# A hybrid of conv attention, causal attention and a recurrence: the first steps in a stated order, the provisional factor from 31 tiles, and W x of the last tile's first 384 queries in the final chain

## The chip, the cores and the metric

One NeuronCore of a Trainium2 chip runs the whole program. The metric is the device time of one execution in microseconds; the profile adds the span from the first to the last instruction of one execution.

## The reference, cut to what matters

The input `x` is (4, 128, 64, 64), float32: four images of 128 channels and 4096 positions.

```python
x = x + conv_attn(gn(x))          # q, k: 64 channels, v: 128; softmax(q k) over all 4096 positions, no mask
t = tokens(x)                     # (4, 4096, 128)
t = t + attn(ln(t))               # one head of 128, causal, scale 1/sqrt(128)
Wx = ln(t) @ W.T                  # then per channel over all 4 x 4096 tokens:
Wx = (Wx - mean) * rsqrt(var + 1e-5) * gamma + beta
y[l] = sigmoid(Wx[l] + y[l-1] @ V.T)    # scan over the 4096 tokens; V orthogonal
out = t + y
```

Mean and variance of `Wx` need every token of every image, so the scan can't get its final factor and offset before the last tile of the last image has passed both attentions.

## The kernel before, in words

`fast_kernel` does the work; it leaves a flag, and `general_kernel`, a plain version, runs afterwards only if the flag says that the result may not be trusted (`ok`, `good`, `wrong` at its end, L1281 to L1297).

**Tiles.** Tokens lie on the free axis in tiles of 512 queries (`QT`), eight per image (`NQ`). Scores are made for pairs of 128 keys: one unit is (image, layer, tile, pair). `score` (L1038 on) issues the two score products `ps` on TensorE (PE) and the exponential `s` on ScalarE (ACT); `product` issues the product with the values, `av`, and on VectorE (DVE) the running sum `total`. In the causal layer the diagonal blocks are cut by a select on GpSimd (POOL), L1073. `s` has three buffers.

**Start.** `gn_stats` gives the group norm's mean and factor of image 0. `keys0` then makes per tile: the normalised `xg` (DVE, L681), an addition of the value bias to X on POOL (L683), the joint projection `pk` of queries and keys (PE, L686), the keys `k` (ACT, L689) and the queries `QR` (DVE for image 0, L696), the split of the keys in a high and a low part (`kh` L699, `K` L700 and L703), and the values `pv` (PE, L707) with their copy (ACT, L708). `query0` splits the queries in the same way (`qh` L717, `q` L720 and L721). `xg` has two buffers, the small PSUM pool (`misc`) two.

**Between tiles.** Generators of the side work stand in lists, and `step` advances them, one step per unit. A scheduler then orders the instructions of each engine. The last part, `last_part`, stands under `tc.manual_schedule`, where the engines keep the program's order.

**End.** The last tile of image 3 is done in two parts, 384 queries (`LAST`) and 128. `ffn` makes, for each tile, the deviation of every token (`deviations`, `rstd`), spreads it along the free axis (`spread`: seven small copies and a transpose on DVE), multiplies it onto `W x` (`pw`, PE L824; product L825) into `WX`, and gathers statistics. From all tiles but the last 128 queries a provisional ("guess") gain and offset are made (`scale(9, "guess")`); with these the states ahead of each chunk of the recurrence take their first step (`first_step`, ACT L594). `last_part` finishes the last 128 queries, their statistics (`scale(15, "all")`) give the final gain and offset, and the chains of the recurrence start (`seed`, `advance`, L1187, L1202, L1203). Each chunk is warmed up from ten tokens ahead (`WARM`), and `BEHIND` chunks of the last image take their first step with the final factor.

`idle` issues matmuls whose result nobody reads.

Of the kernel before, what the change touches and what calls it, by code (L numbers as in the profile page):

```python
# [25 lines left out]
F32 = mybir.dt.float32  # L26
AF = mybir.ActivationFunctionType
ALU = mybir.AluOpType
# [446 lines left out]
def fast_kernel(  # L475
# [103 lines left out]
        nc.gpsimd.tensor_tensor(dst, dst, mhalf[:, :n], ALU.pow)  # L579

    first = []
    BEHIND = P // CHUNK[-1] - 1

    def shifted(gain, less, base, name):
        bias = const.tile([P, 1], F32, name=f"bias_{name}")
# [10 lines left out]
    with ExitStack() as actx:  # L596
# [75 lines left out]
        def keys0(b, c):  # L672

            if c == 0:
                K0[b] = kv.tile([P, N], F32R, tag="K0", name=f"K0_{b}")
                QR[b] = qr_tile(f"QR_{b}")
                V0[b] = WX[B - 1].rearrange("p l s t -> p (l s t)").rearrange("p (n c) -> p n c", c=C)
            xn = tmp.tile([P, QT], F32, tag="x", name=f"xg_{b}_{c}", bufs=2)
            gmv, grs = gn[b]
            xt = X[b][:, ts(c, QT)]  # L680
            nc.vector.tensor_scalar(xn, xt, gmv[:, 0:1], grs, ALU.subtract, ALU.mult)  # L681

            nc.gpsimd.tensor_scalar(xt, xt, B0v, None, ALU.add)  # L683
            yield
            pk = misc(f"pk_{b}_{c}")
            nc.tensor.matmul(pk, lhsT=W0qk.rearrange("p h o -> p (h o)"), rhs=xn, start=True, stop=True)  # L686
            k = tmp.tile([P, QT], F32, tag="k", name=f"k_{b}_{c}")
            low, up = slice(0, CQ), slice(CQ, P)
            nc.scalar.activation(k[up, :], pk[up, :], AF.Identity, bias=B0qk[up, :])  # L689
            half, col = divmod(c, NQ // 2)  # L690
            rows = QR[b][ds(half * CQ, CQ), ts(col, QT)]
            if b:

                nc.scalar.activation(rows, pk[low, :], AF.Identity, bias=B0qk[low, :])
            else:
                nc.vector.tensor_scalar(rows, pk[low, :], B0qk[low, :], None, ALU.add)  # L696
            yield
            high = tmp.tile([P, QT], F32, tag="h", name=f"kh_{b}_{c}", bufs=2)
            nc.vector.tensor_scalar(high[up, :].bitcast(I32), k[up, :].bitcast(I32), HIGH, None, ALU.bitwise_and)  # L699
            nc.vector.tensor_tensor(K0[b][up, ts(c, QT)], k[up, :], high[up, :], ALU.subtract)  # L700
            if b:
                yield
            nc.scalar.copy(K0[b][low, ts(c, QT)], high[up, :])  # L703
            yield
            pv = misc(f"pv_{b}_{c}")
            for j in range(4):
                nc.tensor.matmul(pv[:, ts(j, P)], lhsT=xn[:, ts(j, P)], rhs=W0v, start=True, stop=True)  # L707
            nc.scalar.copy(V0[b][:, 4 * c : 4 * c + 4, :], pv.rearrange("p (j c) -> p j c", j=4))  # L708
            yield

        def query0(b, c):

            half, col = divmod(c, NQ // 2)
            rows = ds(half * CQ, CQ)
            src = QR[b][rows, ts(col, QT)]
            high = tmp.tile([P, QT], F32, tag="h", name=f"qh_{b}_{c}", bufs=2)
            nc.vector.tensor_scalar(high[rows, :].bitcast(I32), src.bitcast(I32), HIGH, None, ALU.bitwise_and)  # L717
            q = qp.tile([P, 2, QT], F32R, tag="q", name=f"q0_{b}_{c}")
            for h in range(2):
                nc.scalar.copy(q[ds(h * CQ, CQ), h, :], high[rows, :])  # L720
                nc.vector.tensor_tensor(q[ds((1 - h) * CQ, CQ), h, :], src, high[rows, :], ALU.subtract)  # L721
            Q[b, 0, c] = q
            yield

# [75 lines left out]
        def ffn(b, c, off, w):  # L800
            name = f"f_{b}_{c}_{off}"
            cols = ds(c * QT + off, w)
            src = X2[b][:, cols]
            if b < len(kept):
                nc.sync.dma_start(out=kept[b][:, cols], in_=src)
            yield
            if (b, c) == (B - 1, NQ - 1):
                pt = misc(f"pt_{name}")
                for j in range(w // P):
                    nc.tensor.transpose(pt[:, ts(j, P)], src[:, ts(j, P)], ident)  # L810
                tok = pt.rearrange("p (j c) -> p j c", c=C)
            else:
                tok = yield from turn(src, None, name, ("f", b, c, off))
            _, rstd = deviations(tok, w // P, 1e-5, name)
            yield
            pw = misc(f"pw_{name}")[:, :w]

            part = WX[b][:, :, ds((c * QT + off) // CHUNK[b], w // CHUNK[b]), :].rearrange("p l s t -> p s l t")

            def chunks(row):  # L820
                return row.rearrange("p (s l t) -> p s l t", l=CHUNK[b] // 2, t=2)

            rb = spread(rstd, name)
            nc.tensor.matmul(pw, lhsT=FWc, rhs=src, start=True, stop=True)  # L824
            nc.vector.tensor_tensor(part, chunks(pw), chunks(rb), ALU.mult)  # L825
            if w == QT:
                nc.vector.bn_stats(stats_f[:, b * NQ + c, :], WX[b][:, :, ts(c, QT // CHUNK[b]), :])
                yield
                return
            nc.vector.bn_stats(groups[:, 3:9], WX[b][:, :, ds(c * QT // CHUNK[b], LAST // CHUNK[b]), :])  # L830
            yield
            whole(("most",))
            gain, less = scale(9, "guess")
            scales["guess"] = gain, shifted(gain, less, Fb0, "guess")
            yield

        scales = {}

        def scale(n, name):

            mv = small.tile([P, 2], F32, name=f"mv_{name}")
            nc.vector.bn_aggr(mv, groups[:, :n])
            gain = const.tile([P, 1], F32, name=f"gain_{name}")
            rsqrt(gain, mv[:, 1:2], 1e-5, 1)
            less = const.tile([P, 1], F32, name=f"less_{name}")
            nc.vector.tensor_scalar(less, mv[:, 0:1], -1.0, None, ALU.mult)
            nc.vector.tensor_tensor(gain, gain, Fgamma, ALU.mult)
            return gain, less

        def most_stats():  # L850

            for k in range(NQ - 1):
                whole(("f", B - 1, k, 0))
            mv = small.tile([P, 2], F32, name="mv_most")
            nc.vector.bn_aggr(mv, stats_f.rearrange("p c s -> p (c s)"))
            nc.vector.tensor_copy(groups[:, 1:2], mv[:, 0:1])
            nc.vector.tensor_scalar(groups[:, 2:3], mv[:, 1:2], float(B * N - QT), None, ALU.mult)
            yield

        def last_tokens():  # L860
# [3 lines left out]
            scales["tok"] = tok = small.tile([P, C], F32, name="tok_last")  # L864
            nc.scalar.copy(tok, pt[:, :P])
            yield

        def last_part(av, pz, s):

# [9 lines left out]
                first_step(b, 0, NC[b] - 1, scales["guess"])  # L879
            rz = small.tile([P, 1], F32, name="rz")  # L880
            nc.vector.reciprocal(rz, pz[:, 0:1])
            ptok = wide[0][:, 0, :w]
            nc.tensor.matmul(ptok, lhsT=avs, rhs=W1v, start=True, stop=True)
            prz = wide[1][:, 0, :w]
            nc.tensor.matmul(prz, lhsT=rz.to_broadcast([P, P]), rhs=ident, start=True, stop=True)
            po = misc("po_last")[:, :w]
            nc.tensor.matmul(po, lhsT=W1v, rhs=avs, start=True, stop=True)
            idle(misc("idle_last"), 3)
            tok = scales["tok"]
            nc.vector.scalar_tensor_tensor(tok, ptok, rz, tok, ALU.mult, ALU.add)  # L890
            rzs = tmp.tile([P, QT], F32, tag="b", name="rzs")[:, :w]
            nc.scalar.copy(rzs, prz)
            for b in range(2, B):
                first_step(b, 0, NC[b] - 1 - (BEHIND if b == B - 1 else 0), scales["guess"])
            stats = small.tile([P, 6], F32, name="lst_last")
# [5 lines left out]
            nc.vector.scalar_tensor_tensor(rzs, rzs, GUARD, po, ALU.mult, ALU.mult)  # L901
            x2 = X2[B - 1][:, cols]
            nc.vector.scalar_tensor_tensor(x2, rzs, 1.0 / GUARD, xt, ALU.mult, ALU.add)
            pw = misc("pw_last")[:, :w]
            nc.tensor.matmul(pw, lhsT=FWc, rhs=x2, start=True, stop=True)
            prow = wide[0][:, 1, :w]
# [1 line left out]
            idle(misc("idle_last2"), 2)  # L908
            raw = tmp.tile([P, QT], F32, tag="a", name="raw_last")[:, :w]
            nc.scalar.copy(raw, pw)  # L910
            part = WX[B - 1][:, :, ds((N - P) // CHUNK[-1], P // CHUNK[-1]), :]
            nc.vector.tensor_tensor(
                part.rearrange("p l s t -> p s l t"),
                *[t.rearrange("p (s l t) -> p s l t", l=CHUNK[-1] // 2, t=2) for t in (raw, prow)], ALU.mult,
            )
            nc.vector.bn_stats(groups[:, 9:15], part)
            scales["all"] = scale(15, "all")

        def finish(b, layer, c, off, w, av, total):

# [117 lines left out]
        def score(i):  # L1038
            b, layer, c, off, w, u, n = units[i]
            if u == 0:  # L1040
                if off == 0:
                    begin_tile(b, layer, c)
                else:
                    put(("most",), most_stats())
                    put(("tok",), last_tokens())
                st[b, layer, c, off] = {}
            if (b, layer, c) == (0, 0, 0) and u % 2 == 0:
                whole(("k0", 0, u // 2))
            q = Q[b, layer, c]
# [89 lines left out]
            pass  # L1139
        for k in range(NQ):  # L1140
            put(("k0", 0, k), keys0(0, k))
        whole(("k0", 0, 0))
        put(("q0", 0, 0), query0(0, 0))
        for i in range(len(units) + 1):
            if i < len(units):
                score(i)
# [200 lines left out]
```

## Time and profile before

| | |
|---|---|
| Three runs | 2507.52, 2508.29, 2508.2 us; median 2508.2 |
| The profiled execution | 2507.61 us |
| Its span, first to last instruction | 2505.9 us |
| Around the span | 1.7 us |
| Mean granted TensorE clock | 0.997 |
| Busy: PE, DVE, ACT, POOL | 99%, 71%, 45%, 8% |
| Instructions | 22483 |

The profile comes from one execution. A row of the timeline gives start, length, engine, line, operation, what is written from what, shapes, and in brackets the idle time of the engine before the row with what ended it. "PEld" are weight loads. A float32 matmul is two rows of the trace, one of `K` and `q` in layer 0 (a rounded type) is one. The chain is followed back from the last instruction, each step to what released it. In the stretches, the number in brackets is the count of instructions and the columns after POOL are the granted clock, the DMA engines' share and GB/s.

### The profile page before, as it was taken

To read this page: it belongs to the slowest core of one execution; us is meant where nothing else is said; L and a number is where in the kernel's file an instruction comes from. 1 tells how busy PE (TensorE), PEld (TensorE's weight loads), DVE (VectorE), ACT (ScalarE), POOL (GpSimd) and SP (SyncE) were. 2 spreads that over 40 slices of the span, in tenths; PEclk is the share of its full clock that TensorE was granted. 3 is DMA by queue.
4 is the path that set the end of the run, shared out by engine and by line. 5 is a ranking of instruction groups with operands and counts; after the bars stand their busy time and mean duration, and the time that the engine had idled before them with its cause. 6 is when DMAs were issued, how large, how long until landed. Compare 5 with 4: busy or idle time off the path is not lost.

```text
span 2505.9 us, 22483 instructions
## 1 busy us (share of the span) xinstructions
PE 2469.1 (99%) x7341; PEld 1339.8 (53%) x7341; DVE 1779.4 (71%) x3580; ACT 1138.7 (45%) x1421; POOL 206.9 (8%) x281
## 2 busy tenths in 40 slices
PE   7999999999999999999999999999999999999997
PEld 4555554444555555444555555544455555544465
DVE  6776669655987667856687676876578676786667
ACT  4444444444444444445444444444444444443456
POOL 2010001210000100110000010121010000010000
PEclk9999999999999999999999999999999999999999
DMA  2000001100100000110010000101010000010023
GB/s 75 9 17 9 17 9 38 26 21 13 49 15 9 17 9 18 38 26 13 24 45 13 13 9 18 34 26 26 13 47 17 9 16 10 13 30 17 9 74 138
DMA packets 154079, 64.41 MB, mean 26 GB/s; under 512 B 136160, under 2 KB 136928, under 8 KB 152160
## 3 DMA queue, kind: packets, MB, share of 16 engines
q1 hardware_dynamic: 151344, 59.27, 8.8%
q10 hardware_dynamic: 2608, 3.61, 0.4%
q8 instruction: 60, 0.98, 0.2%
q14 instruction: 67, 0.55, 0.1%
HBM read 31.66 MB, written 31.20 MB: 25 GB/s over the span
## 4 chain that ended last, share of the span: by engine, by line
PE 91%; DVE 5%; ACT 2%; issue 1%; POOL 0%; DMA 0%; SPq 0%; DVEq 0%; POOLq 0%; ACTq 0%
PE av L1108 51%; PE ps L1064 19%; PE ps L1057 16%; PE pv L707 1%; PE pw_f L824 1%; PE po L956 1%; DVE total L1105 1%; PE pk L686 1%; PE pq L794 1%; ACT WX L1203 1%; ACT states L1203 0%; PE pz L1202 0%; ACT WXp L1203 0%; DVE o L941 0%; DVE rb L771 0%
## 5 line engine op out<-in xcount | busy, mean ns | idle before, releaser
L1105 DVE TENSOR_TENSOR total<-total,s 128x1024 f32<-128x1024 f32 (+5 forms) x809 | 882.6, 1094 | 538.3 <-ACT s L1066 290.2
L1108 PE MATMUL av<-s,WXp 128*128 128x512 f32 x2048 | 962.0, 592 | 0.0
L1066 ACT ACTIVATE s<-ps,shift 128x1024 f32<-128x1024 f32 x512 | 570.2, 1115 | 762.2 <-PE ps L1064 743.7
L1064 PE MATMUL ps<-q,K 128*128 128x512 f32 x2048 | 757.9, 492 | 1.4 <-DVE K L700 1.2
L1070 ACT ACTIVATE s<-ps,zero,R 128x512 f32<-128x512 f32 (+3 forms) x607 | 405.8, 719 | 513.4 <-PE ps L1057 507.8
L1108 PEld LDWEIGHTS av<-s,WXp 128*128 128x128 f32 x2048 | 384.3, 188 | 304.0 <-issue 262.8
L1064 PEld LDWEIGHTS ps<-q,K 128*128 128x128 f32 x2048 | 386.2, 189 | 289.9 <-issue 231.1
L1108 PE MATMUL av<-s,V 128*128 128x512 f32 (+3 forms) x1214 | 504.4, 538 | 0.3 <-POOL s L1073 0.3
L1057 PE MATMUL ps<-q,X 128*128 128x512 f32 (+3 forms) x1214 | 503.5, 537 | 0.0
L1057 PEld LDWEIGHTS ps<-q,X 128*128 128x128 f32 x1214 | 224.9, 190 | 236.3 <-issue 219.5
L1108 PEld LDWEIGHTS av<-s,V 128*128 128x128 f32 x1214 | 223.6, 190 | 229.9 <-issue 205.4
L579 POOL TENSOR_TENSOR rstd<-rstd,mhalf 128x4 f32<-128x4 f32 x32 | 32.4, 1012 | 1024.4 <-DVE rstd L578 1024.4
L1073 POOL TENSOR_SCALAR_AFFINE_SELECT s<-s 128x128 f32<-128x128 f32 x128 | 48.7, 385 | 540.9 <-ACT s L1070 540.0
L579 POOL TENSOR_TENSOR rstd_f<-rstd_f,mhalf 128x4 f32<-128x4 f32 (+1 forms) x32 | 47.3, 1480 | 382.8 <-DVE rstd_f L578 362.3
L683 POOL TENSOR_SCALAR X<-X,B0v 128x512 f32<-128x512 f32 x32 | 64.6, 2021 | 141.5 <-DVE xg L681 140.0
L786 DVE TENSOR_SCALAR V<-V,lmv,rstd 128x128 f32<-128x128 f32 x128 | 38.7, 345 | 37.0 <-POOL rstd L579 36.9
L721 DVE TENSOR_TENSOR q<-QR,qh 64x512 fp32r<-64x512 f32 x64 | 44.1, 688 | 6.8 <-PE ps L1064 5.6
L924 DVE TENSOR_TENSOR t<-total 128x512 f32<-128x512 f32 x64 | 44.0, 688 | 4.2 <-PE pfw L638 2.5
L926 DVE STREAM_TRANSPOSE tt<-t 128x512 f32<-128x512 f32 x64 | 45.2, 707 | 1.7
L939 DVE STREAM_TRANSPOSE rb<-z 128x512 f32<-128x512 f32 x64 | 44.8, 700 | 0.9
L941 DVE SCALAR_TENSOR_TENSOR o<-rb,av 128x512 f32<-128x512 f32 x64 | 43.6, 681 | 2.3
L932 DVE COPY side<-part 32x16 f32<-32x16 f32 (+1 forms) x256 | 41.3, 161 | 3.9
(187 smaller groups left out, 1233.6 us busy)
## 6 DMA issues: line engine op xcount, KB each, us to landing
turn<-t SPq DMA_DIRECT2D x32, 256.0 KB, 2.0
V<-turn SPq DMA_DIRECT2D x128, 64.0 KB, 2.6
turn_f<-t_f SPq DMA_DIRECT2D x31, 256.0 KB, 2.0
t_f<-turn_f SPq DMA_DIRECT2D x124, 64.0 KB, 2.6
X<-in_x SPq DMA_DIRECT2D x28, 256.0 KB, 4.7
kept<-X SPq DMA_DIRECT2D x24, 256.0 KB, 2.0
Y<-kept SPq DMA_DIRECT2D x6, 1024.0 KB, 7.7
out<-Y SPq DMA_DIRECT2D x5, 1024.0 KB, 6.0
```

Of the source, the lines that this page charges most:

```text
L579: nc.gpsimd.tensor_tensor(dst, dst, mhalf[:, :n], ALU.pow)
L683: nc.gpsimd.tensor_scalar(xt, xt, B0v, None, ALU.add)
L721: nc.vector.tensor_tensor(q[ds((1 - h) * CQ, CQ), h, :], src, high[rows, :], ALU.subtract)
L926: nc.vector.transpose(tt, t)
L939: nc.vector.transpose(rb, z[:, :k].unsqueeze(2).to_broadcast([P, k, 32]))
L1057: nc.tensor.matmul(ps[:, h, first[h] : w], lhsT=lhsT, rhs=q[:, off + first[h] : off + w], start=True, stop=True,)
L1064: nc.tensor.matmul(ps[:, h, :], lhsT=lhsT, rhs=q[:, k, :], start=k == 0, stop=k == 1)
L1066: nc.scalar.activation(s, ps, AF.Exp, bias=shift)
L1070: nc.scalar.activation(part, ps[:, h, first[h] : w], AF.Exp, scale=scale, bias=zero)
L1073: nc.gpsimd.affine_select(out=edge, in_=edge, pattern=[[1, P]], base=0, channel_multiplier=-1, compare_op=ALU.is_ge, fill=0.0,)
L1105: nc.vector.tensor_tensor(t, t, s[:, h, f:w], ALU.add)
L1108: nc.tensor.matmul(av[:, first[h] : w], lhsT=V[:, 2 * u + h, :], rhs=s[:, h, first[h] : w], start=u == 0 and h == 0, stop=2 * u + h == n - 1,)
```

## The change

Three parts.

1. The first steps of `keys0` and `query0` of image 0 are issued in a stated order under `tc.manual_schedule` for DVE, ACT and PE: `xg_0`, `xg_1`, then `pk_0` with its reads, the first half of the queries' split, the keys' split, the second half, `pv_0` with its copy, `xg_2`, and `pk_1` with its reads. For the very first tile the queries are read out of `pk` ahead of the keys.
2. The provisional gain and offset come from the 31 full tiles (`most_stats`) and no longer from the first 384 queries of the last tile as well. `most_stats` starts at unit 11 of these 384 queries instead of at the beginning of the last 128. `BEHIND` goes from 3 to 15, the chunks of the whole last tile.
3. For the 384 queries, `ffn` ends with `rstd` and the product `pw`, left in a PSUM bank of the `av` pool. The row of deviations is made in `last_part` by three matmuls of the broadcast `rstd` with the identity (`row`), copied by ACT (`rows`), and multiplied onto `pw` with the statistics behind it (`write_last`), ahead of the same two operations for the last 128. One idle matmul ahead of the last `av` takes the place of three behind `po`.

```diff
-    BEHIND = P // CHUNK[-1] - 1
+    BEHIND = QT // CHUNK[-1] - 1
...
+            for read in (queries, keys) if (b, c) == (0, 0) else (keys, queries):
+                read()
...
             for h in range(2):
                 nc.scalar.copy(q[ds(h * CQ, CQ), h, :], high[rows, :])
                 nc.vector.tensor_tensor(q[ds((1 - h) * CQ, CQ), h, :], src, high[rows, :], ALU.subtract)
+                if (b, c, h) == (0, 0, 0):
+                    yield
...
             _, rstd = deviations(tok, w // P, 1e-5, name)
             yield
+            if w < QT:
+                pw = ps_av.tile([P, QT], F32, tag="av", name=f"pw_{name}")[:, :w]
+                nc.tensor.matmul(pw, lhsT=FWc, rhs=src, start=True, stop=True)
+                scales["early"] = pw, rstd
+                yield
+                return
...
-            nc.vector.bn_stats(groups[:, 3:9], WX[b][:, :, ds(c * QT // CHUNK[b], LAST // CHUNK[b]), :])
-            yield
-            whole(("most",))
-            gain, less = scale(9, "guess")
-            scales["guess"] = gain, shifted(gain, less, Fb0, "guess")
...
             mv = small.tile([P, 2], F32, name="mv_most")
-            nc.vector.bn_aggr(mv, stats_f.rearrange("p c s -> p (c s)"))
+            gain, less = scale(mv, stats_f.rearrange("p c s -> p (c s)"), "guess")
+            yield
+            scales["guess"] = gain, shifted(gain, less, Fb0, "guess")
...
+        def write_last(off, w, row, pw):
+            part = WX[B - 1][:, :, ds((N - QT + off) // CHUNK[-1], w // CHUNK[-1]), :]
+            nc.vector.tensor_tensor(
+                part.rearrange("p l s t -> p s l t"),
+                *[t.rearrange("p (s l t) -> p s l t", l=CHUNK[-1] // 2, t=2) for t in (row, pw)], ALU.mult,
+            )
+            k = 9 if off else 3
+            nc.vector.bn_stats(groups[:, k : k + 6], part)
...
             nc.vector.reciprocal(rz, pz[:, 0:1])
+            idle(misc("idle_last0"), 1)
...
-            idle(misc("idle_last"), 3)
...
             nc.scalar.copy(rzs, prz)
+            pw_early, rstd_early = scales["early"]
+            row = wide[1][:, 1, :LAST]
+            for j in range(LAST // P):
+                nc.tensor.matmul(
+                    row[:, ts(j, P)], lhsT=rstd_early[:, j : j + 1].to_broadcast([P, P]), rhs=ident, start=True, stop=True
+                )
...
+            rows = tmp.tile([P, QT], F32, tag="r", name="rows_early")[:, :LAST]
+            nc.scalar.copy(rows, row)
+            write_last(0, LAST, rows, pw_early)
             pw = misc("pw_last")[:, :w]
...
-            nc.vector.bn_stats(groups[:, 9:15], part)
-            scales["all"] = scale(15, "all")
+            write_last(LAST, w, raw, prow)
+            scales["all"] = scale(mv, groups, "all")
...
-                    put(("most",), most_stats())
                     put(("tok",), last_tokens())
+            if (b, layer, c, off, u) == (B - 1, 1, NQ - 1, 0, 11):
+                put(("most",), most_stats())
...
-        whole(("k0", 0, 0))
         put(("q0", 0, 0), query0(0, 0))
+        key0, key1, key2, query = ("k0", 0, 0), ("k0", 0, 1), ("k0", 0, 2), ("q0", 0, 0)
+        engines = {mybir.EngineType.DVE, mybir.EngineType.Activation, mybir.EngineType.PE}
+        with tc.manual_schedule(engines=engines):
+            for key in (key0, key1, key0, query, key0, query, key0, key2, key1):
+                next(made[key])
```

## The prediction

> **What bounds the kernel now.** I read the page's busy shares first, then the chain that ended last, then the timeline of the two places that the change touches, and the busy time by stretch for the clock.
>
> ```profile
> PE 2469.1 (99%) x7341; PEld 1339.8 (53%) x7341; DVE 1779.4 (71%) x3580; ACT 1138.7 (45%) x1421; POOL 206.9 (8%) x281
> ```
>
> TensorE is busy 99% of the span. So only what makes PE wait, or runs while PE is not the bound, can give time; the change touches two such places, the first scores (14 to 26 us) and the last attention tile with the chain behind it (2404 to 2438 us). In the timeline of the start the bracket is the idle time before the row:
>
> ```profile
> 14.03 2.07 PE L686 MATMUL pk<-xg,W0qk 128*128 128x512 f32 x2 [1.66 <-DVE xg L681]
> 15.90 1.92 PE L707 MATMUL pv<-W0v,xg 128*128 128x128 f32 x8
> 18.49 2.08 PE L686 MATMUL pk<-xg,W0qk 128*128 128x512 f32 x2 [0.68 <-ACT WXp L708]
> 20.36 1.92 PE L707 MATMUL pv<-W0v,xg 128*128 128x128 f32 x8
> 21.92 2.68 PE L1064 MATMUL ps<-q,K 128*128 128x512 f32 x8
> 24.44 1.02 PE L686 MATMUL pk<-xg,W0qk 128*128 128x512 f32 x2
> ```
>
> PE pauses once, 0.68 us before the second `pk`. A `pk` takes 2.08 us at 14 and 18 us and 1.02 us at 24 us: the clock is half until about 23.2 us. In the chain near the end, by start, length and work:
>
> ```profile
> 2428.80 0.41 DVE total L1105
> 2429.21 0.12 DVE mv_guess L842
> 2429.35 0.15 DVE gain_guess L578
> 2429.50 0.07 DVE less_guess L846
> 2429.58 0.72 POOL gain_guess L579
> 2430.30 0.68 POOL ok L1281
> 2430.98 0.26 POOL s L1073
> 2431.24 0.04 issue
> 2431.29 0.50 PE av L1108 x2
> 2431.81 0.30 DVE avs L875
> ```
>
> The last causal select (POOL s L1073) stands behind the guess's power and a memset in POOL's order, and these behind DVE's work on the 384 queries. Its scores left ACT at 2429.31, so 1.6 us of the chain is queueing. Busy time by stretch (us, PE, PEld, DVE, ACT, POOL, PEclk):
>
> ```profile
> 16.36:19.78 3.42, 2.75 (x9) 1.93 (x9) 1.87 (x4) 1.30 (x3) 2.34 (x2) 1.00 0.00 0
> 19.78:23.19 3.41, 3.41 (x12) 2.66 (x12) 3.32 (x6) 2.89 (x5) 0.43 (x2) 1.00 0.00 0
> 2429.59:2433.00 3.41, 2.50 (x19) 2.33 (x20) 1.36 (x6) 2.34 (x5) 1.64 (x3) 1.00 0.10 19
> 2433.00:2436.42 3.42, 3.30 (x10) 1.88 (x9) 1.77 (x9) 1.23 (x4) 0.55 (x1) 0.50 0.94 347
> ```
>
> The 1.00 of the first two rows is not real, as the `pk` durations show. The last row is: half clock while the final chain runs.
>
> **The start, step by step.** The stated order puts `QR`, `qh`, half of `q`, `kh`, `K`, the other half ahead of `xg_2` on DVE, where `xg_2` now waits 3.42 us for `pv_0` and holds `QR` until 18.31. After `pk_0` (16.11): `QR` 0.73, then `k` on ACT 0.68 behind it (the built order makes `k` wait for `QR`), so `pk_0` is read out at 17.6. In the built order `pk_1` waits for that, no longer for the copy of `pv_0` (end 18.44); `pv_0` ends at 17.82, so the pause goes: -0.7. `pk_1` ends at 19.9. DVE meanwhile needs 0.73 + 0.42 + 0.69 + 0.42 + 0.69, with gaps 3.2 us: `K` at 19.3. `qh` took 0.80 when it ran beside POOL's `X` L683, which would make it 19.7, still under cover of `pk_1`; without that cover it costs what passes 19.9. So the scores start at 19.9, not 21.9. `pv_1` moves behind them, so PE does the same work in another order and the 2.0 us are not all kept; on PE only the pause counts.
>
> What is queued behind moved steps: `pk_2`, needing `xg_2` (now last on DVE), comes after `av_0` and the second scores, at 24 us; POOL's `X` L683 follows `xg_2`, and the copy L505 that starts the next image's loads follows the fifth `total`, at 36.8, and moves with it.
>
> The clock: before, PE worked without a pause from 18.49 and was at full speed 4.7 us later. After, it works without a pause from 14.03. By the same 4.7 us full speed comes at 18.7, and the 4.5 us between hold half of their work too much: -2.2. The other end is no earlier clock, 0. A change in the beat of 3.42 us (the length of the half-clock stretch 2433.00 to 2436.42, and counted back from 23.19) comes at 19.8: -1.7. The row above says that 2.75 busy of 3.42 did not suffice; after, that stretch has 3.4 of 3.42, like the one that did. I take -1.6. Start: **-2.3**, ends -0.3 (the pause alone, and 0.4 of it lost in waiting for the first exponentials) and -2.9.
>
> The Trainium skill, TensorE: Matmul & The Clock Gate, "What's actually happening", says that one busy window of about 3.4 us, in a beat that does not start with the kernel, releases the half clock. By it the clock would come between 17.4 and 20.9 us, an estimate, and the start would be -1.9 to -3.6; the row agrees in so far as 18.49 to 23.19 holds one such whole window.
>
> **Middle.** The guess now needs 31 tiles: aggregation 0.99, 0.15, 0.07, two copies, POOL's power 0.72 for which DVE waits, 0.16, 0.22, at about 2404 to 2406.5. Behind it on DVE stand the `total` additions (0.96 each in a unit of 2.58 us, 1.62 us idle between them now, and `s` has three buffers); behind it on POOL the selects, first due at 2409.57. Both covered by about 3 us: 0; without cover, up to the 1.2 us of stall. `pw` of tile 6 and `pt_last` only move up on PE: 0.
>
> **The tail.** Removed from DVE after 2424: seven copies (1.19 us), transpose 0.58, product 0.56, stats 0.56, and the guess, all between `rstd` and the last `total`. PE is dense until the last scores (2427.99) and stays so. Then:
> - ACT no longer waits 0.56 for `total`: its last scores end 2428.84 (was 2429.31). POOL's memset (0.73) starts with PE's end at 2428.02 and is over at 2428.75; select 2428.87 to 2429.16 (was 2431.23).
> - PE: the last `total` ends 2428.39, `pz` 0.45, one idle matmul 0.23, `av` 0.22, `pz` 0.13, `av` at 2429.44; `avs` at **2429.9** (was 2431.81): -1.9.
> - ACT's table load (1.28) now ends at 2430.14, then `sig` and two first steps at their spacing of 0.11, 0.51, 0.51: `rzs` at 2431.3, 0.3 after its operand. The new matmuls `row` wait for it, with `pw_last` queued behind them on PE: three times 0.22, done 2432.4. The `rows` copy of 384 columns, between 0.27 (128) and 0.59 (512), 0.48: done 2432.9, after the two remaining first steps.
> - DVE: product 0.56 and stats 0.56 (the rows of 2427.52 and 2428.33), then the last product at 2434.0. `x2` (2432.4) and `raw` (2433.0) are ready before; the 1.1 us on DVE, hidden in the 1.45 us for which DVE waits for `last` now, is what is late next. Was 2435.76: **-1.7**. From there to the first recurrence the same instructions; first steps of 15 columns in place of 3: 0.
>
> This has `row` and `pw_last` at full clock; at half, as now, `row` costs 0.7 more: -1.0. The other end is `rzs` straight after its operand, 0.3, and DVE overlapping: -2.1. PE loses two of three idle matmuls; but the stretch that led to half clock had 2.50 of 3.41 busy with many one-column `pz`, and the new one is shorter by the 1.9 us of waiting, so I take full clock.
>
> Sum: -2.3 + 0 - 1.7 = -4.0. The profiled execution took 2507.6 (span 2505.9 and 1.7 around it), 0.6 under the median 2508.2; the four times shown average 2507.9, against which I set it: **2503.9 us**. What a measurement of this kernel can tell from no change is 0.2%, 5.0 us: below 2503.2.
>
> **Rivals.**
> 1. *The half clock at the start lasts to 23.2 as before.* For: 80% busy did not release it. Start -0.3 to -0.7: 2505.7.
> 2. *Half clock in the first recurrences.* For: fewer fillers, and the row at 2429.59 lost the clock. The stretch at half would fall on steps of 1.35 us of ACT work against 1.29 of PE, 2.58 at half: 3.4/2.58 steps lose 1.2 each, 1.6, and 0.7 in the chain. Tail +0.6: 2506.2. Against: six fillers of `py` stand right in front. The Trainium skill, same page and section, has half clock after one idle window of that length, which is this rival; no run here shows how idle it must be.
> 3. *More than the sum.* Clock at 18.7 or before and the tail at its end: -2.9 - 2.1 and below: 2502.7.
> 4. *The provisional factor is too coarse, slower.* The kernel compares the first states' result with the true chunk ends (L1284 to L1297, 2e-6) and else runs the general kernel, at least another 2400 us of PE by the page's 2469: about 5000. It decides when a first state differs so much that nine steps, each of sigmoid slope at most 1/4 and V orthogonal, leave 2e-6, that is by 0.5. Leaving out one tile of 32 can't.
> 5. *The order isn't what it says.* The built order shows `QR` ahead of `xg_2` and the guess ahead of the last additions of the 384 queries: excluded.
>
> **Numbers.** Forecast 0.50, rival 1 0.20, rival 2 0.10, rival 3 0.18, rival 4 0.01, another loss 0.01. The forecast's own range is 2502.6 to 2505.2. Rivals 1 and 2 raise the upper end to 2506.4, rival 3 the lower to 2501.8. Faster by over 0.2%: rival 3 and about a quarter of the forecast, whose lower end passes 2503.2: 0.30. Slower by over 0.2% only in the last two: 0.03. The rest 0.67.
>
> **What would show it.** After: no idle before the second `pk`; scores at 19.9, the `ps` passes at 0.23 apart; `s` of the first tile at 21 to 22; guess power near 2405; select right behind the memset; `avs` 1.9 after the last scores leave PE, not 3.8; the last `WXp` product about 1.7 earlier against the last scores and waiting for DVE's own stats. Wrong if `ps` waits for `q` or `K`, if the `rows` copy waits for ACT, or if clock rows at the end show 0.50.

## Result and the profile after

| | before | after |
|---|---|---|
| median, 22 runs each | 2507.77 us (2507.19 to 2508.67) | 2504.17 us (2503.78 to 2504.76) |
| span of the profiled execution | 2505.9 us | 2502.1 us |

The ratio is 0.9986, with a 95% interval of 0.9980 to 0.9992: 3.6 us less, 0.14%, where 4.0 less (2503.9 us) was predicted. The page of after has PE as before, 99% of the span:

```profile
PE 2466.4 (99%) x7345; PEld 1339.4 (54%) x7345; DVE 1778.1 (71%) x3571; ACT 1137.5 (45%) x1422; POOL 206.9 (8%) x281
```

The timeline of the start of after (start, length, work; in brackets the idle time before it and what ended it):

```profile
14.02 2.07 PE L686 MATMUL pk<-xg,W0qk 128*128 128x512 f32 x2 [1.66 <-DVE xg L681]
16.13 0.74 DVE L697 TENSOR_SCALAR QR<-pk,B0qk 64x512 f32<-64x512 f32 x1 [1.71 <-PE pk L686]
16.91 0.77 DVE L725 TENSOR_SCALAR qh<-QR 64x512 int32<-64x512 int32 x1
17.64 1.48 PE L686 MATMUL pk<-xg,W0qk 128*128 128x512 f32 x2
18.88 0.69 DVE L708 TENSOR_TENSOR K<-k,kh 64x512 fp32r<-64x512 f32 x1
19.71 2.33 PE L1090 MATMUL ps<-q,K 128*128 128x512 f32 x8 [0.60 <-DVE K L708]
```

The second `pk` follows without a pause (17.64, was 18.49 behind 0.68 idle), and half way through it the clock becomes full: 1.48 us, where 2.08 is half and 1.02 full. The scores start at 19.71 (was 21.92), and they now wait 0.60 us for `K` from DVE. The last scores of the last tile start at 2425.29 (was 2427.38). From there, the timeline of the tail:

```profile
2425.96 0.74 POOL L1312 MEMSET ok<- 128x768 f32 x1 [2.94 <-PE ps L1083]
2426.82 0.29 POOL L1099 TENSOR_SCALAR_AFFINE_SELECT s<-s 128x128 f32<-128x128 f32 x1
2428.01 0.29 DVE L895 COPY avs<-av 128x128 f32<-128x128 f32 x1 [1.70 <-PE av L1134]
2429.48 0.93 PE L917 MATMUL last<-ident,rstd_f 128*128 128x128 f32 x6 [0.19 <-ACT rzs L912]
2430.96 0.56 DVE L881 TENSOR_TENSOR WXp<-rows_early,pw_f 128x384 f32<-128x384 f32 x1 [0.45 <-ACT rows_early L932]
2432.03 0.27 DVE L881 TENSOR_TENSOR WXp<-raw_last,last 128x128 f32<-128x128 f32 x1
2434.54 1.21 PE L1233 MATMUL py<-states,FV 128*128 128x255 f32 x4 [0.47 <-DVE py L1218]
```

The select (L1099) stands right behind the memset, `avs` is 3.80 us earlier than before (2.09 of it came with the last scores), and the last `WXp` product waits for no other engine: DVE was at its own product and stats until then. Busy time by stretch (us, PE, PEld, DVE, ACT, POOL, clock) of after:

```profile
14.96:18.38 3.42, 3.42 (x11) 2.46 (x10) 2.18 (x3) 1.30 (x2) 2.44 (x2) 1.00 0.00 0
2431.60:2435.02 3.42, 2.25 (x9) 1.35 (x8) 2.61 (x11) 0.00 (x0) 0.55 (x1) 1.00 1.03 426
```

The recorded clock is full from 18.38 (was 23.19) to 2489.63 without a break: the half-clock stretch at 2433 is gone. Two stretches divide the 3.8 us between the profiles: from the first `pk` to the last scores 2411.27 (was 2413.35), -2.08, and from the last scores to the first recurrence 9.25 (was 10.91), -1.66. The rest is unchanged.

### The profile page after: what moved, and what is told of

It reads as the page before. It is cut to its first block, busy times and chain, and to the rows that moved or that the text cites. A ratio compares the mean times of both kernels' runs of the same rounds, so it can differ in the third digit from the quotient of the medians.

```text
span 2502.1 us, 22482 instructions
## 1 busy us (share of the span) xinstructions
PE 2466.4 (99%) x7345; PEld 1339.4 (54%) x7345; DVE 1778.1 (71%) x3571; ACT 1137.5 (45%) x1422; POOL 206.9 (8%) x281
## 4 chain that ended last, share of the span: by engine, by line
PE 94%; DVE 3%; ACT 2%; issue 1%; POOL 0%; DVEq 0%; POOLq 0%; ACTq 0%
PE av L1134 52%; PE ps L1090 19%; PE ps L1083 17%; PE po L981 1%; PE pw_f L841 1%; PE pq L804 1%; PE pv L715 1%; PE pk L686 1%; ACT WX L1234 1%; DVE total L1131 1%; ACT states L1234 0%; PE pz L1233 0%; ACT WXp L1234 0%; ACT s L1092 0%; DVE stats L649 0%
## 5 line engine op out<-in xcount | busy, mean ns | idle before, releaser
L1099 POOL TENSOR_SCALAR_AFFINE_SELECT s<-s 128x128 f32<-128x128 f32 x128 | 49.0, 387 | 532.8 <-ACT s L1096 531.7
```

What stands on the lines that cost most here:

```text
L1099: nc.gpsimd.affine_select(out=edge, in_=edge, pattern=[[1, P]], base=0, channel_multiplier=-1, compare_op=ALU.is_ge, fill=0.0,)
```

## Experiments

The table has each kernel's median against that of before, timed beside it (2507.77 to 2507.87), and from its profiled execution three lengths and one wait: **A** from the start of the first `pk` to the last scores, **B** from there to the first recurrence matmul `py<-states`, **C** from the cast of `wrong` (the last work before the branch that skips the general kernel) to the end, and the time that PE waits for `K` at about 50 us, which is part of A. Between B and C lie 57.5 us in every kernel of the table but no_idle_last (57.9).

| kernel | time - before | A | B | C | wait at 50 us |
|---|---|---|---|---|---|
| before | | 2413.35 | 10.91 | 10.1 | 0.97 |
| after | -3.6 | 2411.27 | 9.25 | 10.1 | 0.59 |
| start_only | -0.1 | 2411.38 | 12.28 | 11.2 | 0.59 |
| start_again | -0.3 | 2411.37 | 10.76 | 11.2 | 0.59 |
| tail_only | -2.3 | 2412.25 | 9.26 | 10.1 | 0.59 |
| fill_pause | +0.5 | 2413.71 | 11.93 | 10.1 | 0.98 |
| guess31 | +0.2 | 2412.91 | 10.16 | 11.3 | 0.59 |
| prewarm | -4.2 | 2411.75 | 9.25 | 10.1 | 0.98 |
| row_bank | -4.0 | 2411.39 | 8.80 | 10.4 | 0.69 |
| both | -4.7 | 2410.97 | 8.80 | 10.4 | 1.04 |
| start_keep | -0.8 | 2411.57 | 11.68 | 11.5 | 0.78 |
| before_keep | -0.7 | 2412.66 | 10.41 | 10.3 | 0.59 |
| no_idle_last | -3.5 | 2411.30 | 9.53 | 10.0 | 0.59 |

The interval of one ratio is about 0.09% (2.2 us) either way, so a single difference under that isn't established by its ratio alone; what is said of smaller ones rests on the lengths in the traces. These repeat within 0.1 where neither the clock nor the wait at 50 us differs.

**What A holds besides the start.** Of the 2.08 us by which A is shorter in after, 0.38 are not the change's. The scores that start at 42.10 us in before start at 40.69 in after, 1.41 earlier; the next ones are 1.79 earlier (50.34 and 48.55). Between them lies the wait for `K`, here in the timelines of before and of guess31 (described below), which has the old order and the clock of before:

```profile
50.34 2.09 PE L1064 MATMUL ps<-q,K 128*128 128x512 f32 x8 [0.97 <-DVE K L700]
49.98 2.09 PE L1062 MATMUL ps<-q,K 128*128 128x512 f32 x8 [0.59 <-DVE K L700]
```

DVE makes this `K` behind its statistics of the next image. The third to fifth of that image's loads landed at 43.22, 43.89 and 44.57 us in before, and each of these statistics began 0.02 to 0.03 us behind one; in guess31 the loads landed at 42.02, 43.48 and 44.15, and none was waited for. The last column of the table shows both lengths in both orders. Why loads land late in some executions is open. Another 0.20 falls at 1614 us, where PE waits 0.94 for DVE's `o` in before and 0.74 in after; every profile of the old order has 0.94 to 0.97 there and every one of the stated order 0.74 or 0.75, so it goes with the order, though how was not followed. The last 0.1 falls in the last tiles and goes with the provisional factor: guess31 has it, start_only has not.

**The two parts alone.** *start_only* takes the stated order and leaves the tail as before, *tail_only* the reverse:

```diff
 # start_only, against before
-        whole(("k0", 0, 0))
+        with tc.manual_schedule(engines=engines):
+            for key in (key0, key1, key0, query, key0, query, key0, key2, key1):
+                next(made[key])
```

start_only also has the reordered readings of `pk` and the `yield` that the order needs; tail_only has none of these.

> The kernel before with the stated order of the first steps alone; nothing of the tail is changed. Theory (the start gives time in two ways, the pause of 0.68 us before the second pk and an earlier full clock): no idle before the second pk, s of the first tile near 21.5 us instead of 24.01, granted clock recorded full from about 18.4 us instead of 23.19, last scores leave PE 2.1 us earlier than before (2427.38 to about 2425.3), time -2.1 us, ratio near 0.9992. The chain between the last scores and the first recurrence keeps its length: 10.91 us from the start of the last ps to the first py recurrence. Rival A (only the pause counts, the clock is not earned by the order): -0.3 to -0.7 us. Rival B (the two parts depend on each other, the tail gets its clock through the start): the half-clock stretch at 2433 is gone here too, and the time is near that of the whole change, -3.6.

> The kernel after without the stated order of the first steps: the start is as before, the tail as after. Theory (independent parts): first recurrence of py 1.7 us earlier than before (2438.29 to about 2436.6), avs about 1.7 us nearer to the last scores (2.72 us from the start of the last ps instead of 4.43), the half-clock stretch at 2433 gone, time -1.7 us. With start_only the two gains add to that of the whole change, -3.6 to -3.75. Rival (the tail's chain only swaps one wait for another, and what after gained there came from the clock that the start shifted): -0.5 us or less, with a half-clock stretch of about 3.4 us left near 2433.

*Measured.* start_only 2507.71 us, ratio 0.9998 (0.9989 to 1.0007); tail_only 2505.53 us, 0.9990 (0.9981 to 0.9999). The start did what was expected up to the last scores (A is 1.97 shorter than before), and yet the time hardly moved: no theory had that. It was lost in two other places. One is the clock in the tail, here by stretches of start_only:

```profile
2425.34:2428.76 3.42, 1.95 (x17) 1.76 (x15) 2.72 (x10) 2.57 (x5) 1.30 (x2) 1.00 0.00 0
2428.76:2432.17 3.41, 2.96 (x14) 2.75 (x13) 1.28 (x6) 1.78 (x6) 0.35 (x2) 0.50 0.32 79
2432.17:2435.58 3.41, 3.29 (x10) 1.80 (x8) 1.14 (x5) 0.75 (x3) 0.55 (x1) 0.50 0.98 408
```

Half clock for two beats, where before had one (a beat is the fixed 3.41 us at whose edges the granted clock changed in all these traces): B is 1.37 longer. The other is the end, in the timeline of start_only:

```profile
core 0 of [0], span 2506.3 us
...
2495.03 0.14 DVE L1312 CAST wrong<-good 1x1 int32<-1x1 f32 x1
```

11.2 us from the cast to the end of the span, against 10.1 in before and after: C is 1.2 longer. In the trace's branch records VectorE's branch over the general kernel begins 0.35 us behind TensorE's (0.02 in before), and its next record comes 8.35 us after the branch, in before and after about 7.46. The other engines are not later.

**Which loss belongs to the kernel.** *start_again* is start_only once more.

> The stated order alone, the same kernel as start_only once more. Its first trace reached the last scores 2.0 us earlier than before counted from the first pk (2411.38 us against 2413.35), then lost 1.36 on the way to the first recurrence (6.83 us of half clock instead of 3.42) and 1.2 behind the last visible instruction (VectorE's jump over the general kernel ended 8.4 us after it began instead of 7.5). This run tells which of the two losses belongs to the program and which to the run. If the clock's beat is a lottery: its phase is another, and the way from the last scores to the first recurrence is something else between 10.2 and 12.3. If the 1.2 belongs to the program (where its code lies): again 11.3 us from the last cast to the end, and the median is again near 2507.7. If it belongs to the run: 10.1, and the median of these runs falls to about 2506.5.

*Measured.* 2507.61 us. C was 11.2 again, so that cost goes with the built program, as far as two profiles of one program and the table's other programs tell; B was 10.76, without any half clock, so that one is the run's. Why the jump takes longer in this program was not tried. With C put at 10.1, the stated order is worth about -1.3 us on the medians of both, and the two parts add to the whole: -1.3 - 2.3 = -3.6. Each of these medians has the interval of 2.2 us either way, so the sum fits but does not prove the shares.

**The clock without the order.** *fill_pause* fills PE's pause before the second `pk` with useless work of the same kind:

```diff
+            if (b, c) == (0, 0):
+                fill = ps_av.tile([P, QT], F32, tag="av", name="fill")
+                for j in range(2):
+                    nc.tensor.matmul(fill[:, ts(j, P)], lhsT=xn[:, ts(j, P)], rhs=W0v, start=True, stop=True)
```

> The kernel before with two more matmuls behind the first pv, of the same shape and operands, into a tile that nothing reads: at half clock 0.96 us of useless work where PE paused 0.68. The order of all else is that of before. Clock theory (PE's pause kept the clock at half until 23.2): full clock from about 18.4 us in the record; pk_1 starts about 18.8, 0.3 later, and everything behind it runs at full speed, so that the second pk takes about 1.0 instead of 2.08 and s of the first tile comes at about 22.7 instead of 24.0; the time is 1.0 to 1.6 us less than before. Rival (it is the order of DVE's and ACT's first steps, not PE's pause, that makes the scores early; the clock follows something else): second pk still 2.08, full clock at 23.2 or later, time 0.0 to +0.3 us.

*Measured.* 2508.31 us, 1.0002 (0.9993 to 1.0011). The clock came at 18.23 as the theory had it, and gained nothing:

```profile
18.57 1.12 PE L686 MATMUL pk<-xg,W0qk 128*128 128x512 f32 x2
...
22.66 1.64 PE L1068 MATMUL ps<-q,K 128*128 128x512 f32 x5 [1.65 <-DVE q L725]
```

The second `pk` is fast, and PE then waits for `q`, whose chain on DVE starts behind `xg_2`, which waited for the fill, since the fill reads the buffer that `xg_2` is to have. So this run changed more than the clock. tail_only shows the same without a filler, since in its profiled execution the old order happened to get the full clock at 16.96:

```profile
18.13 1.12 PE L686 MATMUL pk<-xg,W0qk 128*128 128x512 f32 x2 [0.68 <-ACT WXp L708]
21.55 0.70 PE L1080 MATMUL ps<-q,K 128*128 128x512 f32 x2 [1.41 <-DVE q L721]
```

In the old order a fast PE pauses twice, 0.68 and 1.41 us. So the rival (the order counts) was right: at an early clock in both, the order is worth A = 2412.25 - 2411.27 = 1.0 us, by shorter pauses (0.2 of it the one at 1614 us); the clock alone is worth little, since DVE's chain is late.

All profiles together say the same. In the stated order the scores start 5.69 or 5.70 us behind the first `pk` whether the full clock comes for good at 16.14 (prewarm) or at 19.55 us (no_idle_last); what changes is PE's wait for `K` before them: 0.95 us in row_bank and prewarm, 0.05 in no_idle_last. In the old order they start 7.88 or 7.89 behind it with the clock at 17.96 (before_keep) as with the clock at 23.19 and 23.25 (before, guess31), and 7.55 with the clock at 16.96. By the scores at 42.10 us, the early clock alone had gained 0.36 us in before_keep and 0.69 in tail_only, the stated order with any of its clocks 1.39 to 1.41 (the kernel *both*, described below, 2.19).

**The guess alone.** *guess31* takes only the guess from 31 tiles (`BEHIND` and the places of `most_stats` and `scale`), with the 384 queries' work left on DVE.

> The kernel before with the provisional factor from 31 tiles alone: W x of the last tile's first 384 queries stays in the units, the first steps stay in their order. It takes the guess's aggregation, power and copies (0.12 + 0.15 + 0.07 us on DVE, 0.72 on POOL) out of the queue in front of POOL's memset and the last causal select, but leaves the seven copies, the transpose, the product and the stats of the 384 queries on DVE between rstd and the last total. Theory (both queues, DVE's and POOL's, hold the select; removing one gives a part): select 0.7 to 1.2 us earlier against the last scores, avs about 0.9 earlier, time -0.6 to -1.2 us. Rival A (the guess on POOL is all of it): avs 1.7 earlier, time -1.7. Rival B (the select waits for the last scores behind DVE's total, not for POOL's queue): 0.

*Measured.* 2507.99 us, but C is 11.3 here too; with C at 10.1 it is -1.0. `avs` comes 3.84 us behind the start of the last scores, before 4.43, after 2.72: so 0.6 of the 1.7 is the guess in POOL's and DVE's queue, and 1.1 the 384 queries' work on DVE. The select itself came 1.5 us earlier (2.02 behind the start of the last scores, before 3.56), more than the theory's 0.7 to 1.2, and yet `avs` gained less than its 0.9, since PE then waits for DVE's last `total`, in the timeline of guess31:

```profile
2429.37 0.61 PE L1091 MATMUL pz_last<-ones,total 128*128 128x1 f32 x4 [1.32 <-DVE total L1103]
```

In after the last `total` delays only the weight load of this product, by 0.16. So both queues count, as the theory said; the time that it forecast (-0.6 to -1.2) is met only with C set aside.

**The clock in the tail.** *before_keep* and *start_keep* put six idle matmuls where PE waits for the last `total`:

```diff
             if last:
+                idle(misc("keep"), 6)
                 pz = misc("pz_last")
```

> The kernel before with the same six idle matmuls. It tells how much of the tail's gain (tail_only 2.3 us) was the clock and how much the shorter queue: theory, first recurrence 10.2 us after the last scores instead of 10.91, no half clock there, median 0.4 to 1.0 below before, so that 1.3 to 1.9 of the 2.3 are the shorter chain. Rival (all of the tail's gain was clock): median 2.0 below before. Rival (none of it): 0.

> start_only with six idle matmuls (1.4 us) on PE where it waited 1.47 us for the last total, between the last scores and the sums of the last token. Nothing waits for them. Theory (a beat with little matmul work there costs the clock, and with it 0.8 to 1.4 us of the final chain): no half-clock stretch between 2428 and 2438, 10.2 us or less from the last scores to the first recurrence instead of 12.27, and the median 0.5 to 1.3 below that of start_only. Rival (the half clock comes whatever PE does there, or costs nothing since the chain waits anyway): the same stretch, median the same.

*Measured.* 2507.17 us (-0.7) and 2507.09 us (-0.8; start_only -0.1, start_again -0.3). before_keep had no half clock and B = 10.41. In start_keep the fillers did not suffice: they ran until 2427.9, a beat began at 2427.25, and half clock followed from 2430.66 to 2434.08 with B = 11.68. So the half clock in the old tail is a matter of where the beat falls: B is 10.8 without it (start_again), 10.9 and 11.7 with one beat (before, start_keep) and 11.9 to 12.3 with two (fill_pause, start_only). That the fillers help is likely by the medians and the trace of before_keep; these two ratios do not settle it.

**The fillers that after kept.** *no_fillers* leaves out one idle matmul behind `rz`, the two of `idle_last2`, and the six that write `py`. That last part changes the computation: `advance` adds its product to a tile (`start=False`) that these six wrote first, so they are not among the matmuls whose result nobody reads. That the states are then no longer added to what VectorE wrote into `py` is a reading of the code; the run shows only that the result failed the kernel's own comparison.

```diff
-            idle(misc("idle_last0"), 1)
...
-            idle(misc("idle_last2"), 2)
...
-                idle(ps.rearrange("p t h s -> p (t h s)"), 1)
+                pass
```

> The kernel after without the idle matmuls of the final chain (one before the last token's first product, two after the last deviation row, six in front of the first recurrence). Rival 2 of the prediction, if the fillers hold the clock: a half-clock stretch of 3.41 us or more between 2428 and 2440, first recurrence up to 0.7 us later and three steps of it slower by 1.2 each, time +0.7 to +2.3 against after, and the spread of its runs as wide as that of before (2.5 us) instead of 1.0. If the shorter wait alone holds it (the beat needs well over half of its 3.41 us without matmul columns, as in the three beats that led to half clock in the traces so far): no half clock, first recurrence 0.0 to 0.4 earlier since nothing stands in front of it, time 0 +- 0.3.

*Measured.* 10759.21 us: the comparison at the kernel's end sent it into the general one, 8255 us over after. Up to that branch the trace still answers the question, by stretches of no_fillers:

```profile
2431.48:2434.89 3.41, 0.00 (x0) 0.00 (x0) 2.64 (x11) 0.08 (x1) 0.55 (x1) 1.00 1.00 418
2434.89:2438.31 3.42, 3.32 (x7) 2.29 (x8) 3.42 (x8) 1.26 (x4) 0.00 (x0) 0.50 1.01 422
```

A beat without any matmul, and half clock in the next, at nearly the phase of after (1.19 us, after 1.31); in after the `py` matmuls were most of the 2.25 us of the stretch at 2431.60 shown above, and the clock stayed. B is 9.27 all the same, but from there to the cast it takes 58.6 us, not 57.5. Rival 2 of the prediction was real: at this phase of the beat the six `py` matmuls hold the clock. *no_idle_last* leaves out only the other three:

> The kernel after without the one idle matmul before the last token's first product and the two after the last deviation row, but with the six that write the first tiles of the recurrences (which, as the run without any of the nine showed, are needed: they make the tile ready to be added to, and without them the comparison at the end sends the kernel into the general one). Theory: the six alone hold the clock (1.63 us in the beat that had 2.25 busy), so no half clock at most phases of the beat; avs 0.2 earlier against the last scores (2.5 instead of 2.72, as without the nine), time -0.2 to +0.2 against after. Rival 2 of the prediction in its weaker form: half clock in some of its runs, the median +0.3 or more, and a wider spread than the 1.0 us of after.

*Measured.* 2504.32 us, within 0.1 of after against before; its runs spread over 1.9 us (after 1.0), and its profiled one had half clock from 2432.77 to 2436.18, 0.3 more in B and 0.4 behind it. At this other phase the six did not suffice. That is the weaker form of rival 2, but without the cost in the median that it named (0.3 or more).

**What is left.** *row_bank* gives the row its own bank and moves the copy ahead of two first steps; *prewarm* puts 18 + 2 + 5 idle matmuls into the normalization; *both* has the two.

```diff
-            row = wide[1][:, 1, :LAST]
+            row = misc("row_last")[:, :LAST]
```

> The kernel after with the row of deviations in a PSUM tile of its own and its copy to SBUF issued ahead of the first steps of images 2 and 3 on ACT. In after the row's matmuls waited for the first step of images 0 and 1 (ACT rzs, 0.19 us idle) since they shared a bank with it. Theory (row, copy, last WXp product are the chain that ends last there): the row starts 0.3 to 0.4 earlier, the last WXp product as much earlier against the last scores (6.7 us from the start of the last ps to about 6.3), first recurrence 0.3 earlier, time -0.3 against after. Rival (DVE's own product and stats, or the product x2, end last): 0.0.

> The kernel after with 18 + 2 + 5 idle matmuls (into a tile that nothing reads) from about 2.5 us on, ahead of and between the small matmuls of the first normalization, so that the full clock is granted before the first pk. What the five traces so far showed: the granted clock changes only at the edges of a beat of 3.41 us whose phase against the kernel's start was another in each run (2.71, 1.31, 1.88, 3.31, 1.17 us), and the first beat in which PE was busy for 2.96 us or more released the half clock, one with 2.73 did not. Theory: first pk 1.0 us instead of 2.07, pv 1.0 instead of 1.91, scores then bound by DVE's chain QR, qh, q, kh, K (3.2 us behind pk_0) and so at about pk_0 + 4.4 instead of + 5.7; time -1.0 to -1.3 against the kernel after, about 2503.0. Rival (the start is bound by DVE's chain and the exponentials, so the clock is worth little here, as the filled pause showed): -0.3 or less against after.

> row_bank and prewarm together, the version that the readings so far point to. If both gains are real and independent: -1.3 to -1.6 us against after, about 2502.7, and about -5 against before. If the start is bound by DVE: -0.3 to -0.6 against after.

*Measured.* 2503.84, 2503.61 and 2503.17 us, which is -0.3, -0.6 and -1.0 against after. In row_bank the row no longer waits, and B is 0.45 shorter:

```profile
2429.28 0.83 PE L917 MATMUL row_last<-ident,rstd_f 128*128 128x128 f32 x6
```

Its last scores start at 2425.44, so the row comes 3.84 behind them, in after 4.19. In prewarm the clock was full from 5.9 to 12.73, half again from 12.73 to 16.14, and the scores started at 5.70 behind the first `pk`, after's 5.69, behind 0.95 of waiting for `K`: its gain is in the median only, and its trace does not show it (A is 0.48 longer than in after, 0.39 of it the wait at 50 us). In the kernel *both* the full clock came back earlier, at 15.38:

```profile
14.28 1.62 PE L693 MATMUL pk<-xg,W0qk 128*128 128x512 f32 x2
...
19.18 2.34 PE L1097 MATMUL ps<-q,K 128*128 128x512 f32 x8 [0.60 <-DVE K L715]
```

The scores start 4.90 behind the first `pk` and again wait 0.60 for DVE's `K`. So row_bank met its theory (-0.3), while prewarm and *both* came out between their theories (-1.0 to -1.3, -1.3 to -1.6) and their rivals. The version *both* is the fastest here, 0.9981 (0.9972 to 0.9989) of before; that it beats after rests on medians 1.0 apart, not on an interval.

## Why the prediction held, point by point

- **Start, -2.3.** The two profiled executions differ by 2.08, within the term's ends, but that is in part luck: 1.4 of it came at the start, 0.38 was the late load in before, 0.2 the wait at 1614 us, 0.1 the provisional factor. The steps held (no idle before the second `pk`, `qh` 0.77 beside POOL, scores at 19.7 for 19.9, `s` of the first tile at 21.48), but two pieces of the working did not. The bound of the scores was DVE's `K`, not the second `pk`, which ended at 19.1 since the clock came at 18.38, before the 19.8 behind the value taken. `ps` waited 0.60 for `K`, which the prediction had named as a sign of being wrong. And the split (pause -0.7, clock -1.6) is not how it works: an early clock without the order gives PE longer waits for `q` (tail_only, before_keep), and with the order an earlier clock only lengthens the wait for `K`. Part of that chain is `qh`: in before and after alike it ended 0.28 us behind POOL's `X` (20.33 behind 20.05, 17.68 behind 17.40), and it took 0.35 more than the 0.42 of `kh`, the same operation on the same shape. Over many runs the term is about -1.3 (the medians, C set aside) or -1.4 (mean A of the four profiles with the old order, fill_pause left out, 2412.79, against 2411.38 of after, start_only, start_again, start_keep, row_bank and no_idle_last), not -2.3. The step that failed is the price of the clock, -1.6. It was taken from one profiled execution of before, in which the old order got the full clock at 23.19 (in those of tail_only and before_keep it got it at 16.96 and 17.96), and as if half-clock work saved on PE were time gained; the runs show PE waiting for DVE in its place.
- **Middle, 0.** Held within 0.1: the guess's power ran at 2403.54, DVE waited 0.48 for it, and the selects from 2408.42 on waited for ACT's exponentials, not for it.
- **Tail, -1.7.** -1.66 between the profiles, with `avs` 1.71 and the last product 1.64 nearer to the last scores, and DVE's own stats as the last thing waited for. Over many runs -2.3 (tail_only, interval -4.8 to -0.3): the sum had the half clock of before at one beat, as in its profile, and the runs have it between none and two (mean B of before, start_only, start_again and fill_pause 11.47, after 9.25). After's tail kept it in every profile but those of no_fillers and no_idle_last, which leave out idle matmuls. So by the median this term was 0.6 too small.
- **The sum.** -4.0 for -3.6: by the medians the start was 1.0 too large and the tail 0.6 too small, for the same reason, one profiled execution of before as the measure of the clock. That the two errors cancel to 0.4 is luck. What the profiles of before and after show (2.08 + 1.66) agrees with the prediction better than what the medians show (1.3 + 2.3), but 0.38 of that 2.08 is the late load.
- **Rivals.** 1 did not come: the beat from 14.96 to 18.38 was busy throughout and full clock followed, and no profile with the stated order got it later than 19.55. The rule of the Trainium skill, TensorE: Matmul & The Clock Gate, "What's actually happening", that a busy beat releases the clock, agrees with 18.38 (the estimate from it was 17.4 to 20.9); so does its remark that the beat does not start with the kernel. But in tail_only the clock came at 16.96, ahead of that estimate, behind a beat with 2.96 us busy of 3.41: here the beat did not have to be busy throughout. 2 was weighed for the right reason: without the six `py` matmuls it happens. The prediction called them fillers, which they are not only. 3 did not come (2504.17, not 2502.7). 4 did not come, but its price was far off: 8255 us more, not some 2500; PE's work in the fast kernel says nothing of the general one's, where one line of four-column matmuls alone is busy for 2396 us and leaves PE idle for 1439 between them.

## What to carry to other kernels

A term that hangs on the granted clock needs more than one profiled execution: the same order got the full clock between 16.96 and 23.25 us. Compare kernels by lengths between two named instructions, ask at several places between them where the difference arose, and look past the last one too: a gain of about 1.3 us was hidden by 1.2 us that another built program paid at its end. Here the stated order was worth what it took off the slower engine's chain, so give PE's clock only the little that this chain leaves it (0.4 to 0.7 us in the old order, nothing to be seen in the new).

## What the runs showed of the hardware

- The granted clock changed only at the edges of a beat of 3.413 us (before: 23.19, 2433.00, 2436.42, 2494.44), whose phase against the kernel's start was spread from 0.37 to 3.31 us over 14 executions.
- PE's busy time did not tell which beats lose the clock: 2.86 us (start_keep) and 2.50 (before) of 3.41 did, 1.94 (start_again) and 2.25 (after) did not. Counting the columns of the matmuls does better, as an estimate: 0.87 ns a column (128-column passes 0.112 us apart), 0.45 for idle matmuls (512 columns in 0.23). The beats of the tails with 39% of columns or less (26, 30, 37, 38, 39) were followed by half clock, those with 43% or more were not; one near the end of fill_pause with 36% was not. At half clock, beats with 82% or more released it, 76% or less did not. The many one-column `pz` matmuls make PE look busy and add next to nothing to this count. The Trainium skill, TensorE: Matmul & The Clock Gate, "What's actually happening", has half clock after one idle beat; here a beat a third full by this count was idle enough.
- The cost of the branch that skips the general kernel (C, cast to end) was 10.0 to 10.4 us in nine profiled executions and 11.2 to 11.5 in four; the program that was profiled twice had 11.2 both times. In start_only and guess31 VectorE alone is late.
